# An additive-attention stage: key-tile steps placed by tables of times, one exponential for two groups, and a PSUM bank shared between numerators and weighted sum

## The chip, the cores and the metric

The kernel runs on one core of one Trainium2 chip. The metric is the device time of one execution in microseconds (us). Three runs of the kernel before took 11651.47, 11655.10 and 11657.09 us; the median is 11655.1 us.

A core has five engines that run side by side, each through its own list of instructions in order: TensorE (PE: matrix products into PSUM, with a load of weights before each), VectorE (DVE), ScalarE (ACT), GpSimd (POOL) and SyncE (SP, which issues transfers here). PSUM has eight banks of 128 x 512 float32. An instruction that needs another engine's result waits for a semaphore, and everything behind it on its own engine waits too.

## The reference

Input x has 4 images of 128 channels by 64 x 64 pixels. A first layer (a convolution and a selective scan) makes x1; the change doesn't touch it. The second layer treats an image as 4096 tokens of 128 channels: attention, then a recurrence, each with a residual. The attention is what the change is about:

```python
def _L1_attn_ref(x, Wt, Wx, bh, Wa, ba):
    q = jnp.einsum('bld,ud->blu', x, Wt)
    k = jnp.einsum('bld,ud->blu', x, Wx)
    beta = jnp.tanh(q[:, :, None, :] + k[:, None, :, :] + bh)
    alpha = jnp.einsum('bsju,u->bsj', beta, Wa[:, 0]) + ba[0]
    alpha = jnp.tanh(alpha)
    alpha = jax.nn.softmax(alpha, axis=-1)
    c_r = jnp.einsum('bsj,bjd->bsd', alpha, x)
    return c_r
...
t = t + _L1_attn_ref(_ln_t(t), L1_attn_Wt, L1_attn_Wx, L1_attn_bh, L1_attn_Wa, L1_attn_ba)
```

For every query s and key j, 32 hidden units are squashed by tanh, weighted and summed, squashed again, and a softmax over the 4096 keys weighs the tokens.

## The kernel before

The kernel has three stages in a row: layer 0 (`_layer0`), the attention (`_rational`) and the recurrence (`_chunked`). A general version behind a flag isn't run with these inputs. All stages are under a manual schedule: each engine gets its instructions in the order in which the Python code emits them.

The attention avoids 32 tanh per pair of query and key. The tanh of a sum is a ratio of exponentials, so a sum of several weighted tanh is one ratio of two products; the 32 units are put in groups of 6, 6, 5, 5, 5 and 5 units. Each group's denominator D and numerator N, for a tile of 128 keys by 512 queries, is one matmul of exponentials of the keys (`F`) with exponentials of the queries (`E`, and `cE` where the weights are multiplied in). A group of 6 takes 64 rows of the array, a group of 5 takes 32 rows. The code handles the groups in three pairs, called units: A (64 rows + 64 rows), B1 (rows 0 to 63 as 32 + 32) and B2 (rows 64 to 127 as 32 + 32). Matmuls on different rows run beside each other.

Work is laid out as 4 images x 8 blocks of 512 queries x 32 tiles of 128 keys (`jt`). For one tile:

- `lower("A"|"B1"|"B2")`, called dA, dB1, dB2 here: two matmuls of denominators into a pair of banks `pd` (two such pairs, four banks).
- `upper(...)`, called nA, nB1, nB2: two matmuls of numerators into two banks `pn`. The pool `npsN` has three banks in turn; the eighth bank, `ct`, is the weighted sum's.
- `inverse`: 1/D as Exp(-Ln(D)), two ACT instructions over 128 x 1024 (lines 1231 and 1232), one pair for each unit.
- `times`: r = r x N, two DVE instructions of 128 x 512 that read a `pn` bank (line 1227).
- two POOL additions of 128 x 1024 (A + B1 at line 1346, + B2 at line 1333), then one DVE addition of the two halves into the scores `A[:, jt, :]` (line 1343, called f below).

Unit B2 of a tile is finished in the next pass of the loop ("late"). The loop fixes the order on each engine: ACT gets Ln A, Exp A, Ln B1, Exp B1, Ln B2, Exp B2. PE gets dA(j), nB2(j-1), dB1(j), nA(j), dB2(j), nB1(j). Then come the extras of `between[jt]`.

After 31 or 32 tiles comes the tail of a block. ACT loads another table and runs Tanh and Exp over the 32 score tiles in four parts (`PARTS`; lines 1381 and 1382, 128 x 2048 to 128 x 6144 each). PE adds weight times token into `ct` (line 1357) for the first 20 tiles. Meanwhile tile 0 of the next block is made without ACT (`ahead`, `direct`: six DVE reciprocals at line 1239, each followed by a product at line 1240), and the denominators of its tile 1 (`first`) are put into `pd`. The weighted sum of the last 12 tiles is put off into passes 2 to 13 of the next block, one tile for each pass, then `closing` follows: copy `ct`, sum the weights (a matmul into the `ct` bank), four quarter reciprocals of 128 x 128 (line 1258), one more matmul, the residual and the store. Passes 15 to 20 hold the layer norm of the next image's tokens (`norm_steps`; its last step is a POOL product at line 1164), passes 24 and 26 the exponentials of the next queries (`queries`).

Of the kernel before, what the change touches and what calls it, by code (L numbers as in the profile page):

```python
# [8 lines left out]
F32 = mybir.dt.float32  # L9
AF = mybir.ActivationFunctionType  # L10
ALU = mybir.AluOpType
# [28 lines left out]
QB = 512  # L40
PARTS = ((0, 4), (4, 12), (12, 20), (20, 32))
LAST_PARTS = ((0, 8), (8, 16), (16, 24), (24, 29), (29, 32))
CLOSE_AT = (14, 16, 17, 18, 19, 20, 22)
NORM_AT = (15, 17, 19, 20)
QUERIES_AT = (24, 26)
NOW = 20
REACH = 21.0
LOWER = 2.0**-13
# [997 lines left out]
def _rational(ctx, tc, k, x1, x2, top, Wt, Wx, bh, Wa, ba):  # L1046
# [12 lines left out]
    two = ctx.enter_context(tc.tile_pool(name="ntwo", bufs=2))  # L1059
    sb = ctx.enter_context(tc.tile_pool(name="nsb", bufs=2))  # L1060
    ra = ctx.enter_context(tc.tile_pool(name="nra", bufs=3))
    rb = ctx.enter_context(tc.tile_pool(name="nrb", bufs=4))
    psD = ctx.enter_context(tc.tile_pool(name="npsD", bufs=2, space=PSUM))
    psN = ctx.enter_context(tc.tile_pool(name="npsN", bufs=3, space=PSUM))
    psW = ctx.enter_context(tc.tile_pool(name="npsW", bufs=1, space=PSUM))

    def ln_exp():
        nc.scalar.preload_act_table_set("natural_log_exp_and_others")
# [1 line left out]
    def pd():  # L1070
        return psD.tile([P, 2, QB], F32, name="pd", tag="pd")

    def pn():
        return psN.tile([P, QB], F32, name="pn", tag="pn")

    def pw():
        return psW.tile([P, QB], F32, name="ct", tag="ct")


    w_t = k.load(wp, Wt, [U, P], "w_t")  # L1080
# [62 lines left out]
    def norm_steps(xn, cols, alloc):  # L1143

        xc = xn[:, cols]
        n = cols.stop - cols.start
        held = {}

        def centre():
            ps = alloc()  # L1150
            _mm(nc, ps, k.avg, xc, n)
            nc.vector.tensor_tensor(xc, xc, ps, ALU.subtract)

        def square():
            held["sq"] = rb.tile([P, CH], F32, name="sq", tag="rb")[:, 0:n]
            nc.scalar.activation(held["sq"], xc, AF.Square)

        def rate():
            ps = alloc()
            _mm(nc, ps, k.avg, held["sq"], n)  # L1160
            _rsqrt(nc, held["sq"], ps, k.eps5)

        def scale():
            nc.gpsimd.tensor_tensor(xc, xc, held["sq"], ALU.mult)

        return centre, square, rate, scale

    def keys(F, xn, c, ps, i):

        exponent(ps, w_k, xn[:, blocks[c]], i, F[:, i, blocks[c]], b_k[:, i : i + 1])  # L1170
# [21 lines left out]
        nc.vector.memset(xT[:, c * nt : (c + 1) * nt, 0:1], 1.0)  # L1192

    def queries(E, xn, s, i):
        exponent(pw(), w_q, xn[:, s * QB : (s + 1) * QB], i, E[:, i, :])

    def weigh(E):
        cE = one.tile([P, 2, QB], F32, name="cE")
# [27 lines left out]
        for a in range(2):  # L1226
            nc.vector.tensor_tensor(r[:, a, :], r[:, a, :], ns[a], ALU.mult)  # L1227

    def inverse(d, pool, tag):
        r = pool.tile([P, 2, QB], F32, name=tag, tag=tag)  # L1230
        nc.scalar.activation(r, d, AF.Ln, scale=LOWER)  # L1231
        nc.scalar.activation(r, r, AF.Exp, scale=-1.0)  # L1232
        return r

    def direct(d, ns, pool, tag):

        r = pool.tile([P, 2, QB], F32, name=tag, tag=tag)
        for a in range(2):
            nc.vector.reciprocal(r[:, a, :], d[:, a, :])  # L1239
            nc.vector.scalar_tensor_tensor(r[:, a, :], r[:, a, :], 1.0 / LOWER, ns[a], ALU.mult, ALU.mult)  # L1240
        return r

    def closing(b, s, ct, xr, parts):

        held = {}

        def take():
            held["ct"] = one.tile([P, QB], F32, name="ct_s")
            nc.vector.tensor_copy(held["ct"], ct)

        def denominators():
            held["den"] = pw()
            nc.tensor.matmul(held["den"], den_w, held["ct"], start=True, stop=True)
            held["rec"] = one.tile([P, QB], F32, name="rec")

        def invert(i):
            cols = slice(i * QB // parts, (i + 1) * QB // parts)
            nc.vector.reciprocal(held["rec"][:, cols], held["den"][:, cols])

        def end():  # L1260
            num = pw()
            nc.tensor.matmul(num, fix, held["ct"], start=True, stop=True)  # L1262
            nc.vector.tensor_tensor(held["rec"], held["rec"], num, ALU.mult)
            nc.gpsimd.tensor_tensor(xr, xr, held["rec"], ALU.add)
            nc.sync.dma_start(x2[b, :, blocks[s]], xr)

        return [take, denominators] + [lambda i=i: invert(i) for i in range(parts)] + [end]
# [23 lines left out]
    cE = weigh(E)  # L1291
    start = 0
    first = lower("A", F, 0, E), lower("B1", F, 0, E)
    between = {}
    for c in range(1, nq):
        for i in range(2):
            between.setdefault(2 * c - 2 + i, []).append(lambda c=c, i=i, xn=xn: keys(F, xn, c, pw(), i))
    for c in range(nq):
        between.setdefault(16 + c, []).append(lambda c=c, xn=xn: turn(xT, xn, c))
    for b in range(B):  # L1300
        upcoming = None
        for s in range(nq):
# [4 lines left out]
            if b + 1 < B:  # L1307

                if s == 0:
                    upcoming = two.tile([P, L], F32, name="xn")  # L1310
                norm_load(b + 1, upcoming, blocks[s])
                for at, go in zip(NORM_AT, norm_steps(upcoming, blocks[s], pn)):
                    between.setdefault(at, []).append(go)
            if more:
                E_next = two.tile([P, 2, QB], F32, name="E")
                of = upcoming if turned else xn
                for i in range(2):
                    between.setdefault(QUERIES_AT[i], []).append(
                        lambda i=i, s=s, of=of, E_next=E_next: queries(E_next, of, (s + 1) % nq, i)
                    )  # L1320
            ln_exp()
            late = None
            for jt in range(start, JT + 1):
                if jt < JT:
                    dA = lower("A", F, jt, E) if jt > start else first[0]
                if late is not None:
                    pj, rA_, rB2_ = late
                    nB2 = upper("B2", F, pj, cE)
                if jt < JT:
                    dB1 = lower("B1", F, jt, E) if jt > start else first[1]  # L1330
                if late is not None:
                    times(rB2_, nB2)
                    nc.gpsimd.tensor_tensor(rA_, rA_, rB2_, ALU.add)  # L1333
                if jt < JT:
                    nA = upper("A", F, jt, cE)
                    rA = inverse(dA, ra, "ra")
                    times(rA, nA)
                    dB2 = lower("B2", F, jt, E)
                    nB1 = upper("B1", F, jt, cE)
                    rB1 = inverse(dB1, rb, "rb")  # L1340
                    times(rB1, nB1)
                if late is not None:
                    nc.vector.tensor_tensor(A[:, pj, :], rA_[:, 0, :], rA_[:, 1, :], ALU.add)  # L1343
                if jt == JT:
                    break
                nc.gpsimd.tensor_tensor(rA, rA, rB1, ALU.add)  # L1346
                rB2 = inverse(dB2, rb, "rb")
                late = jt, rA, rB2
                for go in between.pop(jt, ()):
                    go()  # L1350

            if more:
                E, cE = E_next, weigh(E_next)
# [9 lines left out]
            def ahead(step):  # L1363
                if not more:
                    return
                if step == 0:
                    held["A"], held["B1"] = lower("A", F, 0, E), lower("B1", F, 0, E)
                    held["A"] = direct(held["A"], upper("A", F, 0, cE), ra, "ra")
                elif step == 1:
                    held["B2"] = lower("B2", F, 0, E)  # L1370
                    held["B1"] = direct(held["B1"], upper("B1", F, 0, cE), rb, "rb")
                    nc.gpsimd.tensor_tensor(held["A"], held["A"], held["B1"], ALU.add)
                elif step == 2:
                    held["first"] = lower("A", F, 1, E)
                    r = direct(held["B2"], upper("B2", F, 0, cE), rb, "rb")
                    nc.gpsimd.tensor_tensor(held["A"], held["A"], r, ALU.add)
                else:
                    held["first"] = held["first"], lower("B1", F, 1, E)
# [16 lines left out]
            if more:  # L1395
                nc.vector.tensor_tensor(A[:, 0, :], held["A"][:, 0, :], held["A"][:, 1, :], ALU.add)
                first = held["first"]
                start = 1
            between = {}

            todo = closing(b, s, ct, xr, 4 if more else 1)
            if more:
                for i, jt in enumerate(range(NOW, JT)):
                    between[2 + i] = [lambda jt=jt, weighted=weighted: weighted(jt)]
                for at, go in zip(CLOSE_AT, todo):
                    between[at] = [go]
            else:
                for go in todo:
                    go()
            if turned:  # L1410
                xn = upcoming
                xT = big.tile([P, JT, P], F32, name="xT")
                for c in range(nq):
                    between.setdefault(22 + c, []).append(lambda xT=xT, xn=xn, c=c: turn(xT, xn, c))


@with_exitstack
# [244 lines left out]
```

## Time and profile before

| | |
|---|---|
| median of three runs | 11655.1 us |
| the profiled execution | 11654.41 us |
| its span, first to last instruction | 11652.7 us |
| busy in the span | PE 88%, ACT 82%, DVE 77%, POOL 74% |
| layer 0 | up to about 4000 us |
| attention | about 4000 to 11440 us |
| from the table load of one block's tail to the next block's | 31 times: 223.8 to 230.2 us in an image (228.9 us where shown below), 249, 245 and 243 us where the image changes |
| of it the tail, table load to the first Ln | 31.7 us (49 to 51 us where the image changes) |
| of it 31 tiles | 197.2 us of the 228.9 |

Time is read from the span's start. A line of a timeline gives start, length, engine, line of the code, operation, what it writes and reads, and how many instructions were merged into the line. The brackets at the end give the engine's idle time before it and who ended it. A PE length includes the way through the array, so starts are compared, not lengths. One float32 matmul shows as two passes (x2).

Between the starts of Ln A of two neighbouring tiles, the profile has these times (medians over 31 blocks, us): tile 1 6.02, tile 2 6.15, tiles 3 to 13 6.33 each, 14 to 17 6.16, 6.15, 6.33 and 6.68, tile 19 7.24, tile 22 9.28, tiles 24 and 26 6.48, nearly all others 6.00 to 6.16.

### The profile page before, as it was taken

The page shows a single profiled execution, that of the slowest core. Times are in us where ns is not written, and L with a number is a line of the kernel's source. Part 1 is how long each engine was busy: PE and PEld are TensorE (multiplying, and loading weights), DVE is VectorE, ACT ScalarE, POOL GpSimd, SP SyncE. Part 2 cuts the span into 40 slices and gives each one's busy share as a digit, 9 for nine tenths or more (in the row PEclk, how much of TensorE's full clock was granted, in tenths as well). Part 3 has the DMA queues.
Part 4 walks back from the last instruction along what each step waited for, and adds up shares of the span by engine and source line. Part 5 has one row for each costly group of instructions (what it writes and reads, how often), then busy time and mean ns, then how long its engine had stood idle before and what let it go on. Part 6 is the DMA issues. An engine that isn't in the chain of part 4 may idle for free.

```text
span 11652.7 us, 111820 instructions
## 1 busy us (share of the span) xinstructions
PE 10307.6 (88%) x36210; PEld 3184.3 (27%) x36210; DVE 8997.6 (77%) x10066; ACT 9520.9 (82%) x10209; POOL 8625.1 (74%) x3703
## 2 busy tenths in 40 slices
PE   6787787778777699999999999999999999999997
PEld 2121121122111133333333333333333333333334
DVE  4998899889889677777777777777777777777773
ACT  3566556656655599999999999999999999999996
POOL 3999889889889677767766776767677767776773
PEclk8898898889888799999999999999999999999998
DMA  4888778778778300000000000000000000000001
GB/s 118 189 182 194 171 177 193 170 182 190 179 171 186 79 1 3 6 3 3 6 3 3 3 6 3 3 3 6 3 3 3 6 2 3 3 4 3 2 3 60
DMA packets 225332, 737.77 MB, mean 63 GB/s; under 512 B 41104, under 2 KB 41936, under 8 KB 223712
## 3 DMA queue, kind: packets, MB, share of 16 engines
q1 hardware_dynamic: 221760, 729.96, 26.5%
q8 instruction: 286, 4.69, 0.2%
q14 instruction: 310, 2.54, 0.1%
q10 hardware_dynamic: 2976, 0.58, 0.0%
HBM read 612.95 MB, written 117.44 MB: 63 GB/s over the span
## 4 chain that ended last, share of the span: by engine, by line
PE 50%; ACT 9%; DVE 4%; issue 3%; POOL 0%; DMA 0%; DVEq 0%; POOLq 0%; SPq 0%; ACTq 0%
PE pn L1212 26%; PE pd L1212 16%; PE ct L1357 4%; ACT A L1381 3%; ACT A L1382 2%; DVE rb L1227 2%; ACT rb L1231 1%; ACT rb L1232 1%; PE ct L1134 1%; ACT ra L1231 1%; DVE rb L1239 1%; PE vy L1556 0%; DVE A L1343 0%; PE pn L56 0%; PE ct L1262 0%
## 5 line engine op out<-in xcount | busy, mean ns | idle before, releaser
L1212 PE MATMUL pn<-cE,F 32*128 32x512 f32 (+1 forms) x12288 | 4728.8, 650 | 196.6 <-DVE rb L1227 88.5
L1227 DVE TENSOR_TENSOR rb<-rb,pn 128x512 f32<-128x512 f32 x3972 | 2544.5, 682 | 1310.9 <-PE pd L1212 684.9
L1212 PE MATMUL pd<-E,F 32*128 32x512 f32 (+1 forms) x12288 | 3478.0, 648 | 20.9 <-DVE ra L1239 15.7
L1346 POOL TENSOR_TENSOR ra<-ra,rb 128x1024 f32<-128x1024 f32 x993 | 2634.5, 2653 | 957.2 <-DVE rb L1227 956.9
L1333 POOL TENSOR_TENSOR ra<-ra,rb 128x1024 f32<-128x1024 f32 x993 | 2346.8, 2363 | 409.0 <-DVE rb L1227 348.4
L626 POOL TENSOR_TENSOR dBu<-dtdu,bbcc 128x1024 f32<-128x1024 f32 x1024 | 2398.3, 2368 | 216.9 <-DMA dtdu<-ddd 155.5
L1232 ACT ACTIVATE rb<-rb 128x1024 f32<-128x1024 f32 x1986 | 2099.6, 1057 | 62.8
L1212 PEld LDWEIGHTS pn<-cE,F 32*128 32x128 f32 (+1 forms) x12288 | 1418.0, 185 | 2574.8 <-DVE rb L1227 1066.6
L1231 ACT ACTIVATE rb<-pd 128x1024 f32<-128x1024 f32 x1986 | 2007.6, 1011 | 89.9 <-PE pn L1212 75.2
L668 PE MATMUL py<-h,gather 128*32 128x512 f32 x4096 | 1297.9, 699 | 477.3 <-POOL h L651 364.5
L1227 DVE TENSOR_TENSOR ra<-ra,pn 128x512 f32<-128x512 f32 x1986 | 1317.9, 684 | 231.4 <-ACT ra L1232 175.6
L1212 PEld LDWEIGHTS pd<-E,F 32*128 32x128 f32 (+1 forms) x12288 | 931.4, 185 | 1638.5 <-issue 693.7
L621 ACT ACTIVATE pa<-dtdu,a_neg 128x1024 f32<-128x1024 f32 x1024 | 1145.3, 1119 | 53.1 <-DVE h L641 32.1
L651 POOL TENSOR_TENSOR h<-h,bbcc 128x1024 f32<-128x1024 f32 x384 | 912.0, 2375 | 346.2 <-ACT carry L649 338.5
L641 DVE TENSOR_TENSOR_SCAN pa<-pa,carry,dBu 128x1024 f32<-128x1024 f32 x480 | 1124.7, 2343 | 23.1 <-ACT pa L621 11.3
L1232 ACT ACTIVATE ra<-ra 128x1024 f32<-128x1024 f32 x993 | 1049.6, 1057 | 31.4
L1357 PE MATMUL ct<-A,xT 128*128 128x512 f32 x2048 | 1050.9, 641 | 8.2 <-ACT A L1382 8.2
L1231 ACT ACTIVATE ra<-pd 128x1024 f32<-128x1024 f32 x993 | 1008.7, 1016 | 60.0 <-PE pd L1212 26.5
L649 ACT COPY carry<-pa 128x1 f32<-128x1 f32 x640 | 102.4, 160 | 1043.7 <-DVE h L648 1041.9
L1343 DVE TENSOR_TENSOR A<-ra 128x512 f32<-128x512 f32 x993 | 745.0, 750 | 116.3 <-POOL ra L1333 116.0
L648 DVE TENSOR_TENSOR h<-pa,bbcc 128x1024 f32<-128x1024 f32 x640 | 784.1, 1225 | 59.0 <-PE py L668 0.9
L641 DVE TENSOR_TENSOR_SCAN h<-pa,carry,dBu 128x1024 f32<-128x1024 f32 x288 | 675.0, 2344 | 171.1 <-PE py L668 148.2
(291 smaller groups left out, 8731.3 us busy)
## 6 DMA issues: line engine op xcount, KB each, us to landing
bbcc<-bcd SPq DMA_DIRECT2D x1024, 256.0 KB, 6.9
dtdu<-ddd SPq DMA_DIRECT2D x1024, 256.0 KB, 7.1
ddd<-dd SPq DMA_DIRECT2D x64, 1024.0 KB, 5.1
src<-src SPq DMA_DIRECT2D x64, 512.0 KB, 8.3
xs<-in_x_dram SPq DMA_DIRECT2D x16, 512.0 KB, 7.5
src<-xs SPq DMA_DIRECT2D x16, 512.0 KB, 3.0
bcd<-bc SPq DMA_DIRECT2D x64, 128.0 KB, 2.0
src<-xsT SPq DMA_DIRECT2D x16, 512.0 KB, 5.4
```

What stands on the lines that cost most here:

```text
L621: nc.scalar.activation(dA, its[m].DT[r][:, 0, :], AF.Exp, scale=a)
L626: nc.gpsimd.tensor_tensor(dBu, its[m].DT[r][:, 1, :], its[m].BC[q][:, 0, :], ALU.mult)
L641: nc.vector.tensor_tensor_scan(to[:, step], dA[:, step], live.pop(("dBu", u))[:, step], 0.0 if m % nch == 0 else its[m - 1].carry[:, col : ...
L651: nc.gpsimd.tensor_tensor(h, h, cc, ALU.mult)
L668: nc.tensor.matmul(it.y[to, c], gather, live["h", v][:, c], start=False, stop=(q == QS - 1))
L1212: nc.tensor.matmul(ps[a], F[lo:hi, i, jt * P : (jt + 1) * P], side[lo:hi, i, :], start=True, stop=True)
L1227: nc.vector.tensor_tensor(r[:, a, :], r[:, a, :], ns[a], ALU.mult)
L1231: nc.scalar.activation(r, d, AF.Ln, scale=LOWER)
L1232: nc.scalar.activation(r, r, AF.Exp, scale=-1.0)
L1333: nc.gpsimd.tensor_tensor(rA_, rA_, rB2_, ALU.add)
L1346: nc.gpsimd.tensor_tensor(rA, rA, rB1, ALU.add)
L1357: nc.tensor.matmul(ct, xT[:, jt, :], A[:, jt, :], start=(jt == 0), stop=(jt == JT - 1))
```

## The change

All in `_rational`. The order that the loop spelled out is replaced by two tables of times. `steps` returns each step of a tile with `jt + when[name]`, the extras get times too (`CLOSE_AT`, `NORM_AT`, `QUERIES_AT`, the put-off weighted sums at 1.9, 2.9 and so on), and a block's list is sorted by time (equal times keep the order of the list, in which the extras of the block before come first) and emitted. Only the order of emission follows; nothing waits for a time. Tiles up to 13 use one table, tiles from 14 the other.

Both Ln of B1 and B2 write one buffer of 128 x 2048, and one Exp inverts both (`exB`). The pool of those buffers has 3 of twice the size instead of 4. Tile 0's `direct` uses the same buffers.

The weighted sum's bank becomes the fourth of the numerators' banks: up to time 13.95 of a block `pn` takes three banks in turn, afterwards four, until the block's end. The queries' matmuls and the closing's take `pn` banks instead of `ct`. The closing copies the sum of weights out of PSUM first (one more DVE copy), and the four reciprocals run in SBUF.

```diff
+LATE = 14
+CLOSE_AT = (13.95, 15.9, 16.4, 16.9, 17.4, 17.9, 18.9)
+NORM_AT = (14.9, 16.95, 17.95, 19.95)
+QUERIES_AT = (24.9, 26.9)
+EARLY_STEPS = dict(
+    dB1=-0.50, lnB1=-0.48, dA=-0.33, lnA=-0.29, dB2=-0.10, lnB2=0.01, exA=0.31, exB=0.54, nA=0.65, xA=0.77,
+    nB1=0.79, xB1=1.15, nB2=1.50, xB2=1.56, a1=2.29, a2=2.36, f=2.49,
+)
+LATE_STEPS = dict(
+    dA=-0.44, dB1=-0.23, lnA=-0.12, lnB1=-0.04, exA=0.26, dB2=0.37, lnB2=0.50, nA=0.74, xA=0.81, exB=0.84,
+    nB1=1.11, xB1=1.38, nB2=1.42, xB2=1.49, a1=1.75, a2=1.88, f=2.46,
+)
...
-    rb = ctx.enter_context(tc.tile_pool(name="nrb", bufs=4))
+    rb = ctx.enter_context(tc.tile_pool(name="nrb", bufs=3))
...
-    psN = ctx.enter_context(tc.tile_pool(name="npsN", bufs=3, space=PSUM))
-    psW = ctx.enter_context(tc.tile_pool(name="npsW", bufs=1, space=PSUM))
+    psN = ctx.enter_context(tc.tile_pool(name="npsN", bufs=1, space=PSUM))
...
+    turns = {"taken": 0, "banks": 3}
     def pn():
-        return psN.tile([P, QB], F32, name="pn", tag="pn")
+        i = turns["taken"] % turns["banks"]
+        turns["taken"] += 1
+        return psN.tile([P, QB], F32, name=f"pn{i}", tag=f"pn{i}")
     def pw():
-        return psW.tile([P, QB], F32, name="ct", tag="ct")
+        return psN.tile([P, QB], F32, name="pn3", tag="pn3")
...
+        go["exA"] = lambda: exp(h["ra"])
+        go["xA"] = lambda: times(h["ra"], h["nA"])
+        go["lnB1"] = lambda: log(halves("B1"), h["dB1"])
+        go["lnB2"] = lambda: log(halves("B2"), h["dB2"])
+        go["exB"] = lambda: exp(h["rb"])
+        for u in ("B1", "B2"):
+            go["x" + u] = lambda u=u: times(halves(u), h["n" + u])
+        go["a1"] = lambda: nc.gpsimd.tensor_tensor(h["ra"], h["ra"], halves("B1"), ALU.add)
+        go["a2"] = lambda: nc.gpsimd.tensor_tensor(h["ra"], h["ra"], halves("B2"), ALU.add)
+        go["f"] = lambda: nc.vector.tensor_tensor(A[:, jt, :], h["ra"][:, 0, :], h["ra"][:, 1, :], ALU.add)
+        return [(jt + when[name], f) for name, f in go.items()]
...
         def denominators():
-            held["den"] = pw()
-            nc.tensor.matmul(held["den"], den_w, held["ct"], start=True, stop=True)
+            den = pn()
+            nc.tensor.matmul(den, den_w, held["ct"], start=True, stop=True)
             held["rec"] = one.tile([P, QB], F32, name="rec")
+            nc.vector.tensor_copy(held["rec"], den)
         def invert(i):
...
-            nc.vector.reciprocal(held["rec"][:, cols], held["den"][:, cols])
+            nc.vector.reciprocal(held["rec"][:, cols], held["rec"][:, cols])
...
+            between.append((CLOSE_AT[0], lambda: turns.update(banks=4)))
+            for jt in range(start, JT):
+                between += steps(jt, F, E, cE, A, first if jt == start else None)
+            for _, go in sorted(between, key=lambda e: e[0]):
+                go()
+            turns["banks"] = 3
...
-                    between[2 + i] = [lambda jt=jt, weighted=weighted: weighted(jt)]
+                    between.append((1.9 + i, lambda jt=jt, weighted=weighted: weighted(jt)))
```

Sorted, one tile's share of the lists reads as follows (j is the tile; the other numbers are neighbours in flight).

| engine | tiles 2 to 13 | tiles from 14 |
|---|---|---|
| ACT | lnB2(j), exA(j), lnB1(j+1), exB(j), lnA(j+1) | lnA(j), lnB1(j), exA(j), lnB2(j), exB(j) |
| PE | nB1(j-1), a put-off weighted sum, dB2(j), nB2(j-1), dB1(j+1), nA(j), dA(j+1) | nB1(j-1), dB2(j), nB2(j-1), dA(j+1), nA(j), dB1(j+1) |
| DVE | xB1(j-1), f(j-2), xB2(j-1), xA(j) | xB1(j-1), f(j-2), xB2(j-1), xA(j) |
| POOL | a1, a2 | a1, a2 |

Of the closing, the first and third quarter reciprocals (16.4 and 17.4) come between xB1 and f on DVE; the second and fourth (16.9, 17.9) come behind xA.

## The prediction

> **What bounds the kernel now.** I read the page's busy shares first, then groups of instructions with shapes kept apart in the attention, then timelines by engine for one early tile, one stalled tile and one tail, and busy time by stretches. Layer 0 and the recurrence are untouched, so the answer lies in some 7400 us of attention.
>
> ACT's groups (busy us, mean ns of one):
>
> ```profile
> L1232 ACT ACTIVATE rb<-rb 128x1024 f32<-128x1024 f32 x1986 | 2099.6, 1057 | 62.8
> L1231 ACT ACTIVATE rb<-pd 128x1024 f32<-128x1024 f32 x1986 | 2007.6, 1011 | 89.9 <-PE pn L1212 75.2 <-POOL ra L1333 2.3
> L1382 ACT ACTIVATE A<-A 128x2048 f32<-128x2048 f32 x31 | 59.2, 1910 | 1.0
> ```
>
> Two stretches, an early tile (with a put-off weighted sum) and a late one. The columns are the stretch, its length, then busy us of PE, PEld, DVE, ACT and POOL:
>
> ```profile
> 4563.00:4569.33 6.33, 6.33 (x30) 1.93 (x26) 4.46 (x7) 6.13 (x7) 4.80 (x3) 1.00 0.01 4
> 4850.50:4856.50 6.00, 5.85 (x26) 1.68 (x24) 5.29 (x9) 5.88 (x7) 5.03 (x2) 1.00 0.00 0
> ```
>
> Late tiles take 6.00 us and ACT sets them: three times Ln to its own Exp (1.04 between starts, 31 ns of gap) and Exp to the next Ln (0.96, overlapping 95 ns). Early tiles take 6.33 and PE sets them. Its timeline has no hole:
>
> ```profile
> 4579.51 1.12 PE L1357 MATMUL ct<-A,xT 128*128 128x512 f32 x2
> 4580.56 1.13 PE L1212 MATMUL pd<-E,F 64*128 64x512 f32 x4
> 4581.62 0.70 PE L1212 MATMUL pn<-cE,F 32*128 32x512 f32 x2
> ...
> 4582.69 2.02 PE L1212 MATMUL pn<-cE,F 64*128 64x512 f32 x4
> 4584.65 0.70 PE L1212 MATMUL pd<-E,F 32*128 32x512 f32 x2
> ...
> 4585.84 1.13 PE L1357 MATMUL ct<-A,xT 128*128 128x512 f32 x2
> ```
>
> Starts give the prices: weighted sum 1.05, dA 1.06, nB2 beside dB1 1.07, nA 1.96 (its first half alone 0.90, its second waits for DVE to free a bank, 1.06), dB2 beside nB1 1.19. Sum 6.33. A pass alone is 0.43 (line 1357 streams 11 passes in 4.88 in the tail), so a group of two passes is 0.86 in a stream and 1.06 where the row shape changes.
>
> A third view matters, f (line 1343) against POOL. First an ordinary tile, then a stalled one:
>
> ```profile
> 4568.14 0.69 DVE L1343 TENSOR_TENSOR A<-ra 128x512 f32<-128x512 f32 x1
> 4568.37 2.67 POOL L1346 TENSOR_TENSOR ra<-ra,rb 128x1024 f32<-128x1024 f32 x1 [0.41 <-DVE rb L1227]
> ```
>
> ```profile
> 4879.97 2.84 DVE L1343 TENSOR_TENSOR A<-ra 128x512 f32<-128x512 f32 x1 [0.41 <-POOL ra L1333]
> 4879.90 2.36 POOL L1346 TENSOR_TENSOR ra<-ra,rb 128x1024 f32<-128x1024 f32 x1
> ```
>
> f first: POOL's 2.36 becomes 2.67. POOL first by 0.07: f takes 2.84, until 0.55 after POOL ends, and DVE stands. So they exclude each other, and the first to start wins. Before, f wins by 0.23 in nearly every tile; one loss per block makes tile 22's 9.43 (PE's clock fell to 0.82 over that stretch, too).
>
> **The change, part by part, per block** (before: 31.7 tail + 6.0 tile 1 + 75.8 tiles 2 to 13 + 115.4 tiles 14 to 31 = 228.9).
>
> *ACT, late tiles.* One Exp of 2048 (1.91) replaces two of 1.057. No Ln but lnB2 stands ahead of its own Exp, so the 31 ns gap turns into the 97 ns overlap that independent neighbours show: lnA 0.91, lnB1 0.91, exA 0.96, lnB2 1.04, exB 1.82 = 5.64 (early 5.51). Tiles 14 to 31 before are 18 x 6.00 + 7.4 of extras: 3.4 the lost race, 4.0 layer norm, queries and closing. All stay. 18 x 5.64 + 7.4 = 108.9: **-6.5**. PE needs about 4.7 here (five slots of 0.86, two shape changes of 0.2), which ACT covers; without that cover a late tile would be PE's again. exB makes xB1 wait for both Ln; DVE (6 x 0.605 + 0.6 = 4.2) and POOL (2.36 + 2.67 + 0.2 = 5.2) fit under 5.64.
>
> *PE, early tiles.* Time 1.9 + i equals dB2's time of tile i + 2, and the list puts the weighted sum first, so it stands between nB1 and dB2. They lose each other: nB1 runs alone (rows 0 to 63), dB2 and nB2 use the same rows in turn, and only dB1 runs beside nB2. Slots: nB1 1.06, sum 1.05, dB2 0.86, nB2 with dB1 1.06, nA's first half 0.90 (the second again needs the bank that xB2 frees right after nB2), second half with dA's first beside it 0.86, dA's second 1.05. Sum 6.83, above ACT's 5.51. Eleven cycles and one ACT-bound edge: 80.6, **+4.8**. Bounds: 5.93 if nA's halves go together (-9.9 in eleven tiles), 7.23 if dB2 to nB2 and nA to dA each pay 0.2 (+4.4). I take 6.83, since in the stream of line 1357 neighbours of one shape pay nothing.
>
> The Trainium skill (TensorEngine Tiling (Array Packing), Key Properties) says that a change of tiling mode, not of tile alone, drains TensorE. No row here has two waiting groups of one shape in a row. By that rule the cycle is 6.83; if any waiting group paid, 7.23.
>
> *Lost races.* The quarters at 16.4 and 17.4 stand between xB1 and f (0.95 each, 0.87 between starts). POOL's a1 starts 0.145 after xB1's end, so f comes 0.64 after a1 instead of 0.23 ahead, and ends 2.91 after a1's start instead of 1.33: 1.6 of DVE standing, with xB2 and xA, hence PE's banks, behind it. Twice: **+3.2**. Bounds: 0, if POOL is late too; +3.6 more, if the quarters, now SBUF to SBUF, are locked out themselves.
>
> On that last bound the Trainium skill (SBUF — State Buffer, Who interferes with whom) says that a DVE operation with one SBUF input, outside its two-port modes, doesn't contend with GpSimd. Before, the quarters read PSUM, so no row shows it; by the rule the 3.6 is 0.
>
> The extra copy of the sums (0.68) and the smaller pools I cost at nothing: DVE idles 1.4 in a late tile, and buffers live under three tiles. With that cover gone the copy costs 0.6 per block.
>
> *Tail.* Before, f(31) starts 4.6 after the table load and the six reciprocals at 6.0. ACT needs 31.7 for itself, and its first Ln (A) has had its bank for long. Now exB(31) holds both halves: xB1 1.4, a1 2.4, a2 2.4 put f(31) at 6.3. POOL's slack is 0.4 per tile and the queries' reductions (0.69 each) take it, so a1(31) is queued when a2(30) ends, f(30) loses the race, and xB2(31) is behind it: f(31) at about 9.7, reciprocals from 11.1, ending at 34.8 (five steps of 4.07 and 3.35). lnB1(1) is now ACT's first, and dB1(1) needs the bank of the last reciprocal: 1.1 behind PE's weighted sums as before, 1.1 matmul, Ln B1 at 37.0, Ln A at 37.9: **+6.2**. Bounds: +3.2 without the lost race, +8.5 with PE slowed. Tile 1 then waits for dB2's bank: **+0.9** (0 to 1.5).
>
> *Clock.* The lost race before cost 3.4 where DVE stood 2.15, so 1.3 more. Two more in the tiles, part of it hidden: **+1.3** (0 to 3).
>
> Sum: -6.5 + 4.8 + 3.2 + 6.2 + 0.9 + 1.3 = +9.9 per block, x 31 = 307. On the profiled span of 11652.7 that is 11960; the median is 2.4 above the span and the profiled run 0.7 below the median, far inside the error. Predicted 11960 us.
>
> **Rivals.**
> - *PE pairs its halves* (the other side): early tiles reach ACT's 5.64. 12 x 5.64 is -8.1 instead of +4.8, so -3.0 per block: 11560. It decides from an early tile below about 5.9. For: PE has seven slots where five would do. Against: nA's second half waited in every early tile before, and nA still follows nB2.
> - *f wins its races*: no +3.2, tail +3.2, no clock: +2.4, 11727. For: it won nearly all before. Against: the order on DVE.
> - *f loses in every late tile* once POOL is out of step: about +1.0 in ten tiles, 12270. For: POOL's slack is 0.4. Against: POOL catches up in quiet tiles.
> - *The change doesn't do what it says*: Ln to Exp keeps 1.04 whoever stands between. 3 x 1.04 + 0.96 + 1.82 = 5.90, +4.7 in 18 tiles, 12105. Against: the 95 ns overlap between unrelated neighbours.
>
> **How the numbers follow.** Forecast 0.50; PE pairing 0.13; f winning 0.16; losing everywhere 0.11; no overlap 0.10. The forecast's own bounds (early cycle up, tail down, clock) span 11800 to 12100. The range adds most of f winning and of no overlap: 11700 to 12190. About 0.2% (23 us) is what a measurement of this kernel can tell from no change. Faster is most of the PE rival, 0.11; within 0.2%, 0.04, between it and f winning; slower 0.85.
>
> **What would show it.** Late tiles between extras at 5.64; early tiles at 6.83 with PE full and dB2, nB2 in turn; two f lines of 2.3 us or more per block, each behind one of the quarter reciprocals; first Ln (B1) 37 after the table load. Early tiles under 6, f at 0.69 throughout, or a tail of 32 would prove it wrong.

## The result, and the profile after

The changed kernel takes 12091.5 us (median of four runs, 12089.3 to 12105.2) against 11653.3 us (four runs, 11647.3 to 11657.1): 1.038 times as long, 95% interval 1.036 to 1.040. The profiled execution has a span of 12089.1 us, 436.4 more than the one before. Its parts, from the two traces (means over the 31 stretches from one table load to the next, us):

| | before | after | forecast | measured |
|---|---|---|---|---|
| tail, table load to Ln A | 33.5 | 39.1 | +6.2 | +5.6 |
| tile 1 | 6.0 | 6.2 | +0.9 | +0.2 |
| tiles 2 to 13 | 75.8 | 81.2 | +4.8 | +5.4 |
| tiles 14 to 31 | 114.7 | 116.7 | -2.0 | +2.0 |
| per block | 230.0 | 243.3 | +9.9 | +13.3 |
| 31 blocks | | | +307 | +411 |
| first block of the program, first Ln A to first Tanh | 211.8 | 239.1 | 0 | +27.3 |
| ahead of it, and behind the last | | | 0 | -1.9 |

(The mean tail is longer than the usual 31.7 since it takes in the three changes of image. The forecast for tiles 14 to 31 is -6.5 + 3.2 + 1.3.)

An early tile and a quiet late one in the profile after, in the columns of the stretches shown before (length, then busy us of PE, PEld, DVE, ACT, POOL, then the granted clock):

```profile
4835.48:4842.27 6.79, 6.79 (x29) 2.30 (x27) 4.46 (x7) 5.60 (x7) 5.05 (x3) 1.00 0.01 2
4990.33:4995.96 5.63, 5.63 (x26) 2.06 (x24) 4.32 (x7) 5.60 (x6) 5.40 (x4) 1.00 0.00 0
```

The early tile is PE's, at full clock, with ACT's work down to 5.60; the ten tiles 3 to 12 are 6.78 each. The quiet late tile takes 5.63 and is ACT's. PE counts as busy for all of it too, but the seventh experiment, which changes ACT's list alone, shortens it to 5.55. What an early tile of PE consists of (PE's timeline after):

```profile
4835.46 1.12 PE L1392 MATMUL pn<-A,xT 128*128 128x512 f32 x2
4836.52 1.17 PE L1228 MATMUL pd<-E,F 32*128 32x512 f32 x8
4837.48 2.49 PE L1228 MATMUL pn<-cE,F 32*128 32x512 f32 x7
4839.40 0.59 PE L1228 MATMUL pd<-E,F 64*128 64x512 f32 x1
4839.81 0.59 PE L1228 MATMUL pn<-cE,F 64*128 64x512 f32 x1
4839.83 1.43 PE L1228 MATMUL pd<-E,F 64*128 64x512 f32 x3
4841.19 1.13 PE L1228 MATMUL pn<-cE,F 32*128 32x512 f32 x4
4842.25 0.70 PE L1392 MATMUL pn<-A,xT 128*128 128x512 f32 x1
```

The weighted sum stands by itself (1.06 to the next start), and nB1 ahead of it by itself too (4841.19 to 4842.25, 1.06). The fourth to sixth lines show dA's first half beside nA's second. There is no hole.

Tiles 15 to 17 with the quarter reciprocals (line 1316), VectorE, then GpSimd, then ScalarE:

```profile
4909.83 1.29 DVE L1243 TENSOR_TENSOR rb<-rb,pn 128x512 f32<-128x512 f32 x2 [0.43 <-PE pd L1228]
4911.03 0.95 DVE L1316 RECIPROCAL rec<-rec 128x128 f32<-128x128 f32 x1
4911.90 2.26 DVE L1297 TENSOR_TENSOR A<-ra 128x512 f32<-128x512 f32 x1
4914.08 1.27 DVE L1243 TENSOR_TENSOR rb<-rb,pn 128x512 f32<-128x512 f32 x2
4915.28 1.27 DVE L1243 TENSOR_TENSOR ra<-ra,pn 128x512 f32<-128x512 f32 x2
4916.47 0.94 DVE L1316 RECIPROCAL rec<-rec 128x128 f32<-128x128 f32 x1
```

```profile
4911.26 2.35 POOL L1295 TENSOR_TENSOR ra<-ra,rb 128x1024 f32<-128x1024 f32 x1 [0.83 <-DVE rb L1243]
4915.50 2.35 POOL L1296 TENSOR_TENSOR ra<-ra,rb 128x1024 f32<-128x1024 f32 x1 [1.89 <-DVE rb L1243]
```

```profile
4914.25 1.02 ACT L1246 ACTIVATE ra<-pd 128x1024 f32<-128x1024 f32 x1 [1.42 <-DVE A L1297]
4915.17 0.62 ACT L1172 ACTIVATE sq<-xn 128x512 f32<-128x512 f32 x1
4917.88 1.02 ACT L1246 ACTIVATE rb<-pd 128x1024 f32<-128x1024 f32 x1 [2.09 <-POOL ra L1296]
```

The quarter stands between xB1 and f, POOL starts first by 0.64, and f takes 2.26, to 0.55 behind POOL's end: the race is lost as forecast, at both quarters in all 31 blocks. The last line was not forecast: Ln B1 of tile 17 waits 2.09, and the profile names POOL, not PE. What it lacks is a buffer that an addition frees; the layer norm's `sq` (the line above) holds one of the three.

The tail, VectorE (the table load starts at 5012.96):

```profile
5015.16 2.83 DVE L1297 TENSOR_TENSOR A<-ra 128x512 f32<-128x512 f32 x1 [0.91 <-POOL ra L1296]
5017.91 1.27 DVE L1243 TENSOR_TENSOR rb<-rb,pn 128x512 f32<-128x512 f32 x2
5021.71 0.69 DVE L1297 TENSOR_TENSOR A<-ra 128x512 f32<-128x512 f32 x1 [2.53 <-POOL ra L1296]
...
5023.11 3.35 DVE L1254 RECIPROCAL ra<-pd 128x512 f32<-128x512 f32 x1
...
5043.42 3.35 DVE L1254 RECIPROCAL rb<-pd 128x512 f32<-128x512 f32 x1
```

GpSimd in the same place, a2(30) and a1(31):

```profile
5012.77 2.36 POOL L1296 TENSOR_TENSOR ra<-ra,rb 128x1024 f32<-128x1024 f32 x1
5015.08 2.36 POOL L1295 TENSOR_TENSOR ra<-ra,rb 128x1024 f32<-128x1024 f32 x1
```

a1(31) was waiting when a2(30) ended and starts 0.08 ahead of f(30), so f(30) loses its race (2.83). f(31) comes 8.75 after the table load (forecast 9.7), the reciprocals start at 10.15 (11.1) and end at 33.8 (34.8); Ln B1 starts at 36.2 (37.0) and Ln A at 37.1 (37.9).

f as a whole, from VectorE's groups in the attention:

```profile
L1297 DVE TENSOR_TENSOR A<-ra 128x512 f32<-128x512 f32 x993 | 1067.1, 1075 | 159.7 <-POOL ra L1296 152.7
```

Its mean went from 750 ns (745.0 us in all before) to 1075. Counted in the traces, f takes over 1.4 us 29 times in these 31 blocks before and 208 times after, 6.7 per block: f(14) and f(15), behind the quarters, always, and f(30) in 29 blocks, all as forecast; and besides these f(18) always and f(20), f(21) and f(22) in 16 to 25 of 31. Its excess over 0.69 is 12.2 us per block, 1.9 before. The 146 losses that don't come behind a quarter all have the form of f(30): f waits for the end of a2, and another POOL operation that was already waiting starts first (117 times the next a1, 23 times the layer norm's product, 6 times the closing's addition).

### The profile page after: what moved, and what is told of

The parts are those of the page before. It is cut to its first block, busy times and chain, and to the rows that moved or that the text cites. A ratio compares the mean times of both kernels' runs of the same rounds, so it can differ in the third digit from the quotient of the medians.

```text
span 12089.1 us, 108466 instructions
## 1 busy us (share of the span) xinstructions
PE 10553.1 (87%) x36210; PEld 3556.6 (29%) x36210; DVE 9298.7 (77%) x10098; ACT 9148.2 (76%) x9216; POOL 8596.6 (71%) x3703
## 4 chain that ended last, share of the span: by engine, by line
PE 52%; DVE 7%; POOL 5%; ACT 2%; issue 2%; DMA 0%; POOLq 0%; ACTq 0%; DVEq 0%; SPq 0%
PE pn L1228 23%; PE pd L1228 18%; PE pn L1392 7%; POOL ra L1296 3%; DVE rb L1243 2%; DVE A L1297 2%; POOL ra L1295 2%; DVE ra L1254 1%; ACT rb L1246 1%; PE pn L1150 1%; PE vy L1592 0%; PE pn L68 0%; DVE rec L1316 0%; ACT ra L1246 0%; PE vy L1603 0%
## 5 line engine op out<-in xcount | busy, mean ns | idle before, releaser
L1228 PE MATMUL pn<-cE,F 32*128 32x512 f32 (+1 forms) x12288 | 3831.1, 643 | 264.9 <-DVE cE L1216 174.6
L1228 PEld LDWEIGHTS pn<-cE,F 32*128 32x128 f32 (+1 forms) x12288 | 1357.6, 194 | 2327.5 <-issue 931.7
L1249 ACT ACTIVATE rb<-rb 128x2048 f32<-128x2048 f32 x993 | 1897.0, 1910 | 18.2
L1228 PEld LDWEIGHTS pd<-E,F 32*128 32x128 f32 (+1 forms) x12288 | 1004.8, 192 | 1946.3 <-issue 668.2
L1297 DVE TENSOR_TENSOR A<-ra 128x512 f32<-128x512 f32 x993 | 1067.1, 1075 | 159.7 <-POOL ra L1296 152.7
L1392 PE MATMUL pn<-A,xT 128*128 128x512 f32 x2048 | 1049.2, 640 | 4.5 <-ACT A L1420 4.5
```

Of the source, the lines that this page charges most:

```text
L1228: nc.tensor.matmul(ps[a], F[lo:hi, i, jt * P : (jt + 1) * P], side[lo:hi, i, :], start=True, stop=True)
L1297: go["f"] = lambda: nc.vector.tensor_tensor(A[:, jt, :], h["ra"][:, 0, :], h["ra"][:, 1, :], ALU.add)
L1392: nc.tensor.matmul(ct, xT[:, jt, :], A[:, jt, :], start=(jt == 0), stop=(jt == JT - 1))
```

## The experiments

Unless a line says otherwise, each is one edit of the changed kernel, with one time, and differences are counted from 12091.5; the kernel before took 11654 to 11656 us beside them. The changed kernel's own four times span 16 us, so a single time that differs by less says little. Where an expectation gives 35.8, 34.8, 33.8 or 32.3 us "after the table load" in the tail, the figure counts from the first Tanh; the table load starts 1.3 us earlier, and the other figures (31.7, 10.2, 6.6, 2) count from it.

**The weighted sums behind dB2.**

```diff
-  between.append((1.9 + i, lambda ...: weighted(jt)))
+  between.append((1.95 + i, lambda ...: weighted(jt)))
```

> Only the put-off weighted sums move, from 1.9 + i to 1.95 + i: on TensorE behind dB2(j) instead of ahead of it, so that nB1 and dB2 are neighbours again. If the lost pairing of nB1 with dB2 makes the early tiles 6.78 us (the prediction), tiles 3 to 12 fall to 5.9 to 6.3 us, 5 to 9 us per block, 150 to 280 us in all. Rival, a bank: nA's second half waits for the bank that xB2 frees, whatever stands before it; then tiles stay at 6.6 or more and 60 us at most come back. Rival, the clock: TensorE with gaps gets half its clock, as in the first block of the changed kernel, which has no weighted sum and tiles of 8 to 11 us; then tiles grow to 8 us and the kernel is slower by some 300 us.

11759.3 us, 332 less. Tiles 3 to 12 take 5.94, tiles 2 to 13 69.9 in place of 81.2, which is 11.4 per block; the rest of the block moves by under 1. PE's timeline for a part of one tile:

```profile
4814.22 0.70 PE L1228 MATMUL pn<-cE,F 32*128 32x512 f32 x2
4814.23 0.70 PE L1228 MATMUL pd<-E,F 32*128 32x512 f32 x2
4814.75 0.59 PE L1228 MATMUL pn<-cE,F 32*128 32x512 f32 x2
4814.76 0.59 PE L1228 MATMUL pd<-E,F 32*128 32x512 f32 x2
4815.29 1.13 PE L1392 MATMUL pn<-A,xT 128*128 128x512 f32 x2
4816.34 0.70 PE L1228 MATMUL pn<-cE,F 32*128 32x512 f32 x2
4816.36 0.70 PE L1228 MATMUL pd<-E,F 32*128 32x512 f32 x2
```

nB1 and dB2 start within 0.01 of each other and need 1.07 together, and so do nB2 and dB1. In the changed kernel the same four groups took 1.06 + 0.96 + 0.96: three slots, of which only one held two groups. The forecast's cause of the early tiles is shown: 0.05 in a table of times is worth 2.7% of the kernel.

**The quarter reciprocals behind xA.**

```diff
-CLOSE_AT = (13.95, 15.9, 16.4, 16.9, 17.4, 17.9, 18.9)
+CLOSE_AT = (13.95, 15.9, 16.9, 17.9, 18.9, 19.9, 20.9)
```

> Only the closing's times change: the four quarter reciprocals at 16.9, 17.9, 18.9 and 19.9, all behind xA, none between xB1 and f. If f's lost races come from the quarters and the five or so behind them (tiles 19 to 24) only from POOL being thrown out of step by those, tiles 16 to 18 fall from 23.3 us together to about 19, the losses from 7 to 2 or 3 per block, and 4 to 5 us per block come back, 125 to 155 us. Rival: the later losses are made by the layer norm's POOL product and the queries' reductions; then only the two losses at the quarters go, about 3 us per block, 100 us, and tiles 20 to 24 stay as they are. Rival: f loses there anyway: no change.

12010.4 us, 81 less, under the numbers of the theory and of its first rival. Tile 16 falls from 7.37 to 5.85 and tile 18 from 8.11 to 6.87, but tile 17 stays at 8.4 and tile 20 grows from 6.5 to 7.7. f loses 5.0 times per block: f(14) no more, f(18) in 4 of 31 blocks, but f(19) in 19 (5 before), and f(15), f(20) and f(21) still. The gain is 2.6 per block, where the forecast gave the two quarters 3.2. But f(15) also loses with no quarter between xB1 and it, now to an a1 that was waiting when a2 ended, and most of the later losses are not the quarters' wake. The layer norm's POOL product wins against f(18) in 23 of the changed kernel's 31 blocks. It isn't what makes the others: the eight blocks of the last image, which have no layer norm, lose as often there (7 to 10 per block; 5 to 8 in the others), f(18) included.

**Ln A first in a block.**

```diff
+        if first is not None:
+            when = dict(when, lnA=-0.49)
```

> Only the first tile's Ln A is put ahead of its Ln B1 on ScalarE. If the first Ln waits for the bank of the tail's last reciprocal, which B1 needs and A does not, Ln A starts at 31.7 us after the table load instead of 35.8 and the next tile takes up what is left: Ln B1 stays where it is, and only Ln A and Exp A (2 us) move into the wait, 1 to 2 us per block, 30 to 60 us. Rival: the first Ln of either kind waits for TensorE behind the weighted sums: Ln A stays at 35 or more and nothing is gained.

12012.8 us, 79 less, 2.8 per block. Ln A starts 5.4 behind the end of the second table load in the changed kernel and at once here (30.4 from the first Tanh, not 35.8), while Ln B1 stays where it was (34.8; 34.9 before): the bank of the last reciprocals holds B1 alone. Tile 1, counted from Ln A, grows from 6.2 to 9.8. More came back than Ln A and Exp A, since tile 2 falls from 7.5 to 6.5.

**f(30) and f(31) behind two reciprocals.**

```diff
+        if jt >= JT - 2:
+            last.append(go.pop("f"))
...
                     direct(held["A"], dA, upper("A", F, 0, cE))
+                    while last:
+                        last.pop(0)()
```

> Only f of tiles 30 and 31 moves on VectorE, from ahead of the tail's reciprocals to behind the first two. If the tail is as long as VectorE's six reciprocals behind f(31), they start at about 6.6 us after the table load instead of 10.2, and the tail falls from 35.8 to about 32.3: 3 to 3.6 us per block, 95 to 110 us. Rival: TensorE's weighted sums, which the first denominators stand behind, set the first Ln: under 1 us per block.

12080.0 us, 12 less, inside the 16 us that the changed kernel's own times span: the number is the rival's. VectorE, then GpSimd (table load at 4759.15):

```profile
4759.16 2.48 DVE L1243 TENSOR_TENSOR rb<-rb,pn 128x512 f32<-128x512 f32 x4
4761.56 4.87 DVE L1216 TENSOR_SCALAR cE<-E,c_n 128x512 f32<-128x512 f32 x2
4766.35 3.35 DVE L1254 RECIPROCAL ra<-pd 128x512 f32<-128x512 f32 x1
```

```profile
4761.27 2.37 POOL L1297 TENSOR_TENSOR ra<-ra,rb 128x1024 f32<-128x1024 f32 x1
4763.71 2.43 POOL L1298 TENSOR_TENSOR ra<-ra,rb 128x1024 f32<-128x1024 f32 x1
```

With the two f out of the way, the two products that make cE come while POOL adds, and take 4.87 together; before them they took 0.48 each with POOL idle. The reciprocals start at 7.2 in place of 10.15; by an estimate from these figures (4.87 against 2 x 0.48) they would have started 3.9 us earlier still if POOL didn't exclude this second pair of operations as well. Yet Ln B1 gains 1.3 from reciprocals that start 3.0 earlier, so something behind them holds it too; the last experiment finds it.

**The first three edits together.** 

> The edits of the first three experiments together: weighted sums at 1.95 + i, quarter reciprocals behind xA, the first tile's Ln A first. If the three places are separate, their gains add: 332 + 81 + 79 = 492 us, 11600 us, 0.5% faster than the kernel before. If they are one and the same slack found three times, it stays near the best of them, 11700 us or more.

11623.6 us (eight runs), 0.9975 of the kernel before, interval 0.9964 to 0.9985: faster than it, by 0.25%. The three gains add up but for 24 us (468 of 492), so they are three separate places.

**Three banks for the numerators.**

```diff
-between.append((CLOSE_AT[0], lambda: turns.update(banks=4)))
+between.append((CLOSE_AT[0], lambda: turns.update(banks=3)))
...
-            den = pn()
+            den = pw()
```

(and `pw` in place of `pn` for the closing's second product, the layer norm and the queries)

> Undoes the bank sharing alone: numerators take three banks in turn in all tiles, and the closing's, the layer norm's and the queries' products take the fourth, the weighted sum's, as before. If the extras standing in the numerators' turn cause the late stalls (their DVE readers come late, and nB1 waits for the bank), tiles 16 to 25 fall by several us per block and the kernel is 60 us or more faster. If the fourth bank is what lets the late order run, with nA in line behind nB2 and all three banks taken, tiles 16 to 20 grow and it is 100 to 200 us slower. If banks don't matter, within 30 us.

12333.5 us, 242 more. Tiles 16 to 20 take 8.5, 9.8, 12.2, 10.3 and 7.1 (7.4, 8.4, 8.1, 6.5 and 6.5 with the fourth bank). f loses only three times per block:

```profile
L1297 DVE TENSOR_TENSOR A<-ra 128x512 f32<-128x512 f32 x993 | 854.5, 860 | 96.2 <-POOL ra L1296 96.2
```

The bank that weighted sum and numerators share is thus a gain of this change in its own order, which the forecast didn't price, and the number of lost races alone doesn't tell the time.

**Two exponentials in place of the shared one.**

```diff
-        go["exB"] = lambda: exp(h["rb"])
+        go["exB"] = lambda: exp(halves("B1"))
+        go["exB2"] = lambda: exp(halves("B2"))
...
+        when = dict(when, exB2=when["exB"])
```

> Undoes the shared exponential alone: two Exp of 1024 one behind the other in place of one of 2048. By the prediction's rows the shared one saves 2 x 0.96 - 1.82 = 0.10 us, but makes Ln B2 wait 0.03 and lose 0.09 of overlap to its own Exp. So quiet late tiles should stay within 0.03 of 5.63: the gain of the late tiles comes from the order of Ln and Exp, not from the shared one. xB1 comes 0.9 earlier, the tail shortens by up to 0.9: 0 to 40 us faster. Rival: the shared exponential is what makes the late tile short: then quiet tiles go to 5.73 or more, over 2 us per block, 60 us slower.

12129.9 us, 38 more, so the number missed by its sign. Quiet late tiles take 5.55, not 5.63: the shared exponential is not what makes them short, and two short ones do it even better. What is lost is lost elsewhere: tiles 3 to 12 go from 6.78 to 6.85, and the stalled tiles together grow by more than the quiet ones gain (tiles 14 to 31: +0.6). Why PE's early cycle is 0.07 longer stays open.

**The keys of the first block, twice.** First the products with their readers to another place (2c - 1.3 + i), then the products one tile earlier and the readers 0.6 later:

```diff
-  between.append((2 * c - 1.05 + i, lambda ...: keys(F, xn, c, pw(), i)))
+  for late, go in zip((0, 0.6, 0.62), keys(F, xn, c, pw, i)):
+      between.append((2 * c - 2.05 + i + late, go))
```

> Only the first block: the next image tokens' keys move from 2c - 1.05 + i to 2c - 1.3 + i, behind dA on TensorE, and their DVE reduction from ahead of xB1 to behind xB2. If the 29 us that the first block is longer (tiles 2 to 13 at 8 to 11 us) come from xB1 waiting behind that reduction and from the half clock that TensorE gets in the holes, 20 to 40 us come back, all of it ahead of the first table load at 4287 us. If the tiles are slow since there is no weighted sum to keep TensorE busy, nothing changes.

> Only the first block: each key product stays on TensorE behind dB2, one tile earlier, but its readers move 0.6 of a tile later, the exponential behind the shared exponential on ScalarE, the reduction behind xB2 on VectorE. The eighth experiment moved product and readers together and gained nothing. If what costs 29 us in the first block is that both readers stand at the head of a tile's list and hold ScalarE and VectorE until the product is through TensorE, tiles 2 to 13 fall from 8 to 11 us to 6 to 7, and 20 to 30 us come back. If the cause is TensorE's clock for want of work (no weighted sum in this block), they stay over 8.

12106.8 and 12091.0 us: neither helps, and tiles 2 to 13 of the first block stay at 7 to 11 us in both. In the stretch 4062 to 4110 of the changed kernel PE is granted 0.82 of its clock, in the like stretch of the kernel before 1.00:

```profile
4062.00:4110.00 48.00, 42.77 (x135) 14.44 (x138) 25.14 (x40) 32.10 (x31) 25.80 (x11) 0.82 0.00 0
```

The 27 us of the first block stay unexplained. That its clock is cause and not effect isn't shown.

**The layer norm's squares elsewhere.**

```diff
-held["sq"] = rb.tile([P, 4, QB], F32, name="sq", tag="rb")...
+held["sq"] = room[:, 0, :]      # the next queries' buffer
```

> Only the layer norm's squares move: they go into the half of the next queries' buffer that is still unused, instead of one of the three shared-exponential buffers. In the changed kernel Ln B1 of tiles 17 and 18 starts just behind the end of an a2, with the bank long ready: it waits for a buffer, of which the squares hold one from 16.95 to 19.95. If the three buffers are too few there (the prediction cost the smaller pools at nothing), tiles 17 and 18 lose 1 to 2 us each in the 24 blocks that have a layer norm, 25 to 100 us in all. Rival: the quarter reciprocals' lost races set those tiles and the buffer is only late with them: within 20 us.

12064.8 us, 27 less: the lower end of the expectation, and not far from the rival's 20. The wait it aimed at is gone whole: Ln's groups of B1 and B2 lose all idle time that POOL ended (87.3 us in the changed kernel, first line below; none here, second line):

```profile
L1246 ACT ACTIVATE rb<-pd 128x1024 f32<-128x1024 f32 x1986 | 2027.5, 1021 | 791.8 <-PE pd L1228 703.2 <-POOL ra L1296 87.3
```

```profile
L1249 ACT ACTIVATE rb<-pd 128x1024 f32<-128x1024 f32 x1986 | 2027.6, 1021 | 715.6 <-PE pd L1231 714.2
```

Two thirds of it came back as later waits: tile 17 falls from 8.4 to 7.4, tile 18 grows from 8.1 to 9.1.

**All places, and the tail in another order.** The three edits, the squares, and the tail's list on VectorE: two reciprocals, the products of cE, tile 0's two products with A's numerators, then the two f.

> The fifth experiment's kernel, plus the squares of the ninth, plus the tail in another order: f of tiles 30 and 31 and the two products of cE behind the first two reciprocals. In the fourth experiment those two products took 2.36 and 2.58 us instead of 0.48, since they ran into POOL's additions, which ate what the later f had saved. If that is why the later f gained 11 us and not 100, the reciprocals now start 2 us after the table load, Ln B1 comes 3 us earlier than in the fifth kernel (34.8 after the load), and the time is 11520 to 11560 us. If TensorE behind its weighted sums sets the first Ln B1, the tail gains under 1 us per block: 11600.

11532.1 us (four runs), 0.990 of the kernel before (0.988 to 0.991): the total of the expectation's first case, by other terms. The products of cE take 0.44 each, but Ln B1 comes only 1.0 earlier than in the fifth kernel, not 3, and tail and tile 1 give 0.7 per block. The larger part falls where the squares stood: tiles 14 to 31 are 1.9 shorter than in the fifth kernel, tile 17 alone 1.3 (7.8 to 6.5). In the ninth experiment they were 1.5 shorter; why more comes back here was not tested apart.

**And the first sums ahead of tile 0's numerators** (with the keys' readers of above):

```diff
                     cE = weigh(E)
+                    for jt in range(*PARTS[0]):
+                        weighted(jt)
                     ns = upper("A", F, 0, cE)
```

> The tenth kernel, plus the keys' readers of the eleventh, plus one move in the tail: TensorE gets the first four weighted sums ahead of tile 0's numerators, which wait for cE (now behind two reciprocals), in place of behind them. In the tenth kernel the reciprocals end in time, and yet Ln B1 comes 33.8 us after the table load and tile 1 takes 8.9 us. If TensorE's weighted sums, started late behind the numerators, are what dB1(1) stands behind, Ln B1 comes 2 to 3.4 us earlier: 60 to 105 us, with the first block's 20 to 30: 11400 to 11450 us. If something else holds the first Ln B1, only the first block's part comes: 11500 to 11515.

11482.3 us (four runs, 11470 to 11491), 0.985 of the kernel before (0.983 to 0.986) and 609 us under the changed one. ScalarE's timeline (table load of the tail at 4726.79) shows no wait left ahead of the first two Ln:

```profile
4757.21 1.28 ACT L1079 ACT_TABLE_LOAD   x1
4758.50 1.02 ACT L1260 ACTIVATE ra<-pd 128x1024 f32<-128x1024 f32 x1
4759.42 1.02 ACT L1260 ACTIVATE rb<-pd 128x1024 f32<-128x1024 f32 x1
4760.75 1.02 ACT L1260 ACTIVATE rb<-pd 128x1024 f32<-128x1024 f32 x1 [0.31 <-PE pd L1242]
```

Ln B1 comes 2.5 earlier (31.3 from the first Tanh, 33.8 in the tenth kernel): PE's queue behind cE was the second wait. The gain is 50 us in all, not 60 to 105 for the tail and 20 to 30 for the first block: tail and tile 1 give 2.1 per block, tiles 2 to 31 are 0.8 longer, and the first block, from its first Ln A to the table load, falls by 6.9, from 243.3 to 236.4, about what it is in the changed kernel (237.8).

## Why the prediction was right, and where it was not

The forecast was 11960 with a range of 11700 to 12190, slower at 0.85; the measurement is 12091.5. Sign and main causes were right, the rise is 1.4 times the forecast. The total alone wouldn't show this: the rival without overlap, at 12105, lies nearer to the measurement than the forecast does, and only the profile (5.63 in a quiet late tile, not 5.90) rules it out.

- *ACT, late tiles, -6.5.* The cycle is right: 5.63 in quiet tiles against 5.64, so neighbours do overlap, and the rival without overlap (5.90) is out. The part of it that the forecast gave to the shared exponential was wrong: the order does it, and two exponentials give 5.55.
- *PE, early tiles, +4.8.* Measured +5.4; cycle 6.78 against 6.83. The rival in which PE pairs its halves did not occur in the changed kernel, and moving the sum by 0.05 produced it (5.94). The section Key Properties of the Trainium skill's page "TensorEngine Tiling (Array Packing)" said that only a change of mode drains TensorE; nB2, which waits for dB2's rows in the same shape, follows at 0.96 behind it. Pass by pass, dB2's two start at 4836.52 and 4837.05 and nB2's first at 4837.48: the step from dB2 to nB2 is 0.43, what a pass alone takes, and the 0.10 above the 0.86 of a stream lies inside dB2, where it follows the weighted sum's other shape. So this row agrees with that rule, and 7.23 per tile is excluded.
- *Lost races, +3.2, and clock, +1.3.* This is the step that was mis-sized. The two losses at the quarters and the tail's came as stated, but the forecast then let POOL fall back in step, and f lost nearly three more times per block (6.7, where one old loss, two quarters and the tail make 4). Above 18 quiet tiles, tiles 14 to 31 carried 6.7 us before (114.7 - 18 x 6.00); 6.7 + 3.2 + 1.3 = 11.2 was forecast, and 15.4 is there (116.7 - 18 x 5.63). The further losses have the form that the forecast gave to f(30) alone: a POOL operation is already waiting when a2 ends. So the rival in which f loses whenever POOL is out of step was partly true (behind the extras, not in all late tiles). The half clock grew with it: by the clock records of the traces, PE has half its clock for 11.6 us per block before and 28.7 after, 4.1 and 15.9 of these in tiles 14 to 31. How much of the time is the clock's isn't shown. What puts POOL behind there is not settled: with the quarters and the squares both out of the way (tenth kernel), tiles 14 to 31 still carry 11.9 above quiet tiles, 5.2 more than before, and f(15), f(17) and f(20) lose in nearly every block.
- *The smaller pools, nothing.* Wrong, by 27 us in one run alone and up to 1.9 per block beside the other edits: the forecast counted the tiles' own buffers and forgot that the layer norm's squares take one from the same pool, so Ln B1 waits 2.09 at tile 17.
- *Tail, +6.2, tile 1, +0.9.* Measured +5.6 and +0.2. Each station came 0.8 to 1.0 earlier than forecast, in the order forecast. But the reciprocals are not all that holds Ln B1, as the forecast had it: when they start 3.0 earlier it gains 1.3 (fourth experiment), and with cE behind two reciprocals, PE's weighted sums ahead of the numerators bring it 2.5 forward (last experiment).
- *The quarter reciprocals from SBUF.* The bound of +3.6 is out: 0.94 while POOL adds (4916.47 beside 4915.50), as without it. That agrees with the Trainium skill's page "SBUF — State Buffer", Who interferes with whom.
- *Not in the sum at all:* the first block, +27, and the shared bank, without which the kernel is 242 us slower still. The extra copy of the sums, priced at nothing, was not tested by itself.

## What to carry to other kernels

When a list is ordered by times, look at ties and neighbours: one full-height product between two half-height ones cost 332 us here, and moving it by one place gave that back. A race that one engine wins by 0.2 us is a resource: ask of each instruction that is put ahead of it, and of every other operation that the same partner excludes, who then starts first. And count all users of a pool, not only the loop's own, before calling a smaller one free.

## What the hardware showed that was not expected

- POOL's additions exclude not only f but also cE's TENSOR_SCALAR from SBUF to SBUF: 2.36 on average in the fourth experiment in place of 0.48, while a reciprocal from SBUF to SBUF is untouched (0.94). The section named above lists tensor_scalar among the operations that can enter a two-port mode and then contend with GpSimd; the forecast had looked it up for the reciprocal only.
- PE's timeline after has eight `pd` passes from 4836.52 on, ahead of nB2's. In the list nB2 stands between dB2 and dB1. dB1, whose rows were free, started 0.04 behind dB2 and thus ahead of nB2, which waited for dB2's rows until 4837.48. So TensorE did not start these groups in the order of its list; 332 of the 372 early tiles with a put-off sum show this order, dB2 and dB1 ahead of nB2. The forecast had dB1 beside nB2; the sum is the same within 0.05.
